# A graph layer's edge loop: three tiles of every eighth group copied by columns, in place of one tile of 200 groups

## The chip, the cores and the metric

The kernel runs on one core of a Trainium2 chip. The metric is the time of one execution on the device, in microseconds. The core's engines work side by side, each through a queue of its own in order: PE (matrix products and transposes; PEld is its weight load), DVE (vector work), ACT (scalar work, activations, copies), POOL (here it issues the indirect gathers) and SP (it issues most of the plain transfers). An engine waits for another through semaphores.

## The reference

One message-passing layer with a residual and a layer norm, on 12500 nodes of 64 values and 212500 edges with 32 values each, all in float32. The edges are sorted by their target `dst`.

```python
msg_in = concatenate([x[src], x[dst], edge_attr], axis=-1)      # 64 + 64 + 32
messages = relu(msg_in @ mW1 + mb1) @ mW2 + mb2                 # hidden 128, out 64
aggregated = segment_sum(messages, dst, 12500)
upd_in = concatenate([x, aggregated], axis=-1)
y = x + relu(upd_in @ uW1 + ub1) @ uW2 + ub2
out = (y - mean(y)) / sqrt(var(y) + 1e-5)                       # over the 64 values
```

## The kernel before

**Groups and steps.** The edges are cut into 554 groups of 384 (`GE`), three tiles of 128 each; the last group has 148 edges in two tiles, so there are 1661 tiles. A group goes through three parts, a step or two apart. In `turn`, the rows of `x` that the group's edges point to, which lie one edge per partition in a ring slot `own_s` (20 slots, `RING`), are transposed on PE (L398) into PSUM, and ACT copies the result (L409) into `own_st`, where a group has 384 columns, one per edge: 64 rows of features, then 32 rows of a one-hot that says where in a window of 32 targets the edge belongs; the edge's own values are loaded below these. `hidden` multiplies by the weights (L424, PE) and DVE takes the relu (L435). `sums` adds the group's messages up by target (L452, L457, PE), and DVE adds them to the running sums (L466, L467). Step k is one bundle on PE of turn k, hidden k - 2 and sums k - 4, with one set of waits ahead of it and one signal behind it; in the last ten steps (`SHORT`) the three parts go apart and catch up. As targets are finished, chunks of 512 nodes go through the update (L473 to L521), one piece after each `sums`, the last chunk behind the last group.

**Two ways for the source rows.** Most tiles are fetched from HBM by an indirect DMA that POOL issues, one per tile (`gather`, L165 to L177). It is written 16 steps ahead of its group and may start as soon as ACT has copied the group that had the slot 20 groups earlier (`marks_by`, L672 and L679, holds what its first and later gathers wait for). For some tiles there is no gather. The node features lie transposed in SBUF (`own_xc`), and each edge's column of 64 values is copied from there to its place in `own_st` by an instruction of its own, on ACT (L572) or DVE (L570), with an address that was read into a register (L549). From step 18 (`BEGIN`) on, each step copies 48 columns (`COLS`): 20 on DVE, 28 on ACT. `COPIED` (L87 to L89) lists the groups so served: with 128 columns each there are 200 of them, the first 21, the last 552, one every 2.67 steps. In such a group the first tile comes by columns and the other two are gathered, so ACT's copy of it is two instructions: 32 rows (the one-hot) of the first 128 columns, and all 96 rows of the other 256.

**Order around the change.** In step k, ACT copies turn k, then 28 columns in three parts of 12, 8 and 8, each behind a load of its addresses. DVE does its additions, 5 and 7 and 8 columns, the one-hot of a later group and the relu. The columns of a group are finished in the step before its turn; `hidden`, two steps later, waits for them (L428). The first column of a group on each engine waits until the group that had the place in `own_st` 12 groups earlier has gone through `hidden` (L575).

Of the kernel before, what the change touches and what calls it, by code (L numbers as in the profile page):

```python
# [14 lines left out]
AF = mybir.ActivationFunctionType  # L15
# [5 lines left out]
P = 128  # L21
N = 12500
E = 212500
D = 64
# [5 lines left out]
W = 32  # L30
TG = 3
GE = TG * P
G = (E + GE - 1) // GE
# [14 lines left out]
SHORT = 10  # L48
LEAD = 6
TIMES = 4  # L50
BEGIN = 18
# [3 lines left out]
COLS = sum(VCOLS + ACOLS)  # L55
SPAN = 8
# [3 lines left out]
def tiles_of(g):  # L60

    n = min(GE, E - g * GE)
    return [min(P, n - j * P) for j in range((n + P - 1) // P)]
# [21 lines left out]
TABLE = [(b, min(4, (NP - b) // P)) for b in range(0, NP, CH)]  # L85
FIRST_FREE = 6 + len(TABLE) - 1
COPIED = []  # L87
while BEGIN - (-P * (len(COPIED) + 1) // COLS) < G - 1:
    COPIED.append(BEGIN - (-P * (len(COPIED) + 1) // COLS))  # L89


class Own:
# [23 lines left out]
def ordered(ctx: ExitStack, tc: tile.TileContext, a, own, ok):  # L116
# [3 lines left out]
    nc = tc.nc  # L120
# [20 lines left out]
    columned = set(COPIED)  # L141

    def after(first, *others):

        tc.declare_no_dep(first.ins, group="quiet", reason="waits for the last of a step")
        for i in others:
            tc.add_manual_dep(
                first.ins, i.ins.name,
                mybir.DependencyInfo(mybir.DependencyClass.Sync, mybir.DependencyReason.DATA),
                reason="the kernel's own rings",  # L150
            )
        return first
# [3 lines left out]
    def ordered_by_steps(i):  # L156

        engine = i.ins.engine
        tc.declare_no_dep(i.ins, group="features", keep=before.get(engine, []),
                          reason="TensorE's step has read what the last turn of the ring wrote")  # L160
        tc.add_to_no_dep_group("features", i.ins)
        before[engine] = [i.ins]
        return i

    def gather(g):  # L165
        s = own.s[g % RING]
        loads[g] = [
            nc.gpsimd.indirect_dma_start(  # L168
                out=s[:p, j, :D], out_offset=None, in_=x[:, :],
                in_offset=bass.IndirectOffsetOnAxis(  # L170
                    ap=src_sb[:p, g * TG + j : g * TG + j + 1], axis=0),
            )
            for j, p in enumerate(tiles_of(g)) if j or g not in columned
        ]
        marks = marks_by.pop(g - RING, [])
        for n, i in enumerate(loads[g]):
            after(i, *marks[: n + 1][-1:])  # L177
# [7 lines left out]
    for g in range(AHEAD):  # L185
        gather(g)
# [105 lines left out]
    starts, rows_at, indices, columns_by = {}, {}, {}, {}  # L292
# [46 lines left out]
    def columns(g):  # L339
        t, c = own.st[g // SB % BLOCKS], (g % SB) * GE  # L340
        return t, c, sum(tiles_of(g))
# [50 lines left out]
    def turn(g, ps):  # L392


        s = own.s[g % RING]
        xt = ps[0][: D + W, :GE]
        did = [
            nc.tensor.transpose(xt[:, j * P : j * P + p], s[:p, j, :], ident[:p, :p])  # L398
            for j, p in enumerate(tiles_of(g))
        ]  # L400

        def copy(step):
            t, c, n = columns(g)
            turn_by[g] = step
            whole = [(slice(D + W), slice(n))]
            apart = [(slice(D, D + W), slice(P)), (slice(D + W), slice(P, n))]
            copies = [
                ordered_by_steps(
                    after(nc.scalar.activation(t[r, c : c + n][:, m], xt[r, m], AF.Copy), step))  # L409
                for r, m in (apart if g in columned else whole)  # L410
            ]
            if g >= BLOCKS * SB:
                after(copies[0], hidden_by[g - BLOCKS * SB])
            copy_by[g] = copies
            return copies

        return did, [*loads.pop(g), places_by[g]], copy
# [104 lines left out]

    def indexes(i):

        n = min(SPAN * COLS, P * len(COPIED) - i * SPAN * COLS)
        if n > 0:
            indices[i] = ixp.tile([1, SPAN * COLS], I32, name="index")
            nc.sync.dma_start(indices[i][:, :n], a["src_copied"][:, i * SPAN * COLS :][:, :n])

    def addresses(i):  # L530

        if i in indices:
            t = indices[i][:, : min(SPAN * COLS, P * len(COPIED) - i * SPAN * COLS)]
            nc.vector.tensor_scalar(t, t, 4.0, float(own.at), ALU.mult, ALU.add)

    def registers(k, *parts):

        i, n = divmod(k - BEGIN, SPAN)
        if i < 0:
            return  # L540
        all_parts = [*((ET.DVE, c) for c in VCOLS), *((ET.Activation, c) for c in ACOLS)]
        for part in parts:
            engine, count = all_parts[part]
            c0 = (k - BEGIN) * COLS + sum(c for _, c in all_parts[:part])
            count = min(count, P * len(COPIED) - c0)
            if count <= 0:
                return
            b = c0 - i * SPAN * COLS
            _, v = nc.values_load_multi_w_load_instructions(  # L549
                indices[i][0:1, b : b + count], engines=[engine],  # L550
                min_val=own.at, max_val=own.at + 4 * (N - 1),
                skip_runtime_bounds_check_because="a source is one of the nodes",
            )
            held[part] = engine, c0, v

    def fetch(part, first=None):

        engine, c0, v = held.pop(part, (None, 0, ()))
        if first and v[first:]:
            held[part] = engine, c0 + first, v[first:]  # L560
            v = v[:first]
        for q, at in enumerate(v, c0):
            g, c = COPIED[q // P], q % P
            t, first_c, _ = columns(g)
            o = t.bitcast(U8)[:D, 4 * (first_c + c) : 4 * (first_c + c + 1)]
            x_at = xc_bytes[:D, bass.ds(at - own.at, 4)]
            by = columns_by.setdefault(g, {})
            new = engine not in by
            if engine == ET.DVE:
                by[engine] = nc.vector.tensor_copy(o, x_at)  # L570
            else:
                by[engine] = nc.scalar.activation(o, x_at, AF.Copy)  # L572
            last[engine] = by[engine]
            ordered_by_steps(after(by[engine],
                                   *([hidden_by[g - BLOCKS * SB]] if new else [])))  # L575
# [49 lines left out]
    inputs(1)  # L625
    relative(NEAR_GROUPS, G)
    indexes(0)
    made = summed = 0
    between, held, last = [], {}, {}

    for k in range(G):
# [6 lines left out]
        if k == CHECKED:  # L638
            addresses(0)
            combined()  # L640
            ordered_edges()
            early.close()
            up = ctx.enter_context(tc.tile_pool(name="upd", bufs=2))
# [4 lines left out]
        if k < G - SHORT:  # L648
            between.append(lambda: registers(k, 0))
            step((turn, k), *([(hidden, k - 2)] if k > 1 else []),  # L650
                 *([(sums, k - 4)] if k > 3 else []))
            made, summed = max(0, k - 1), max(0, k - 3)
            if between:
                between.pop()()
        else:

            step((turn, k))
            for _ in range(2):
                if summed < made:
                    step((sums, summed))  # L660
                    summed += 1
            for _ in range(2):
                if made <= k:
                    step((hidden, made))
                    made += 1
            registers(k, 0)
        fetch(0, FIRST)
        registers(k, 1)
        fetch(0)
        window(k + SB)  # L670
        onehot(k + LEAD)
# [346 lines left out]
```

## Time and profile before

| | |
|---|---|
| median of 3 runs | 1869.42 us (1865.05 to 1871.72) |
| profiled execution, its own time | 1870.53 us |
| its span, first to last instruction | 1868.8 us |
| TensorE's granted clock, mean | 0.974 of full speed |
| column copies on ACT / on DVE | 14924 / 10676 |
| DMA, mean busy share between 200 and 1800 us | 0.23 |

How to read it: "busy" counts the time in which an engine has an instruction in work. Loads of registers and the issue of plain DMAs are not counted. A group of instructions carries its line in the kernel, the engine, the tile written and read, the count, the busy time, the mean duration of one, and the idle time of the engine ahead of it with the releaser that the profile infers. Instructions overlap on their engine, so that a column copy with a mean of 192 ns costs ACT about 99 ns (1472.5 us for 14924).

### The profile page before, as it was taken

The numbers are of one execution on the slowest core, as the hardware profiler recorded it, in microseconds if no ns is written. First come the engines' busy times: TensorE is split into PE (matmuls) and PEld (weight loads), VectorE is DVE, ScalarE is ACT, GpSimd is POOL, SyncE is SP. The second block draws the span as 40 slices with busy tenths as digits, with TensorE's granted clock in tenths as the row PEclk, the third lists the DMA queues.
The fourth block names the chain that finished last, engine by engine and source line by source line (L and its number), as shares of the span: only waits on it lengthen the run. The fifth ranks groups of instructions, "written<-read, shape, count | busy, mean of one in ns | idle before, by whom it ended". The sixth has DMA issues, their size and how long they took to land. (4 is left out here: it accounts for less than half of the span.)

```text
span 1868.8 us, 64939 instructions
## 1 busy us (share of the span) xinstructions
PE 1336.8 (72%) x12323; PEld 1171.3 (63%) x12323; DVE 1537.9 (82%) x13355; ACT 1752.3 (94%) x15772; POOL 1386.4 (74%) x1468
## 2 busy tenths in 40 slices
PE   5767767777677677677676776777766767767776
PEld 4766656666666566566665666666656656656665
DVE  4558888888888888888888888888888888888885
ACT  3379999999999999999999999999999999999994
POOL 7777777777777777777777777777777777777771
PEclk9889999999999999999999999999999999999998
DMA  5532222222222222222222222222222222222220
GB/s 143 142 97 61 45 55 54 45 53 51 49 54 45 54 50 50 53 50 50 51 52 50 49 50 49 53 51 49 53 47 53 48 52 53 46 54 49 50 51 15
DMA packets 112209, 103.99 MB, mean 56 GB/s; under 512 B 51267, under 2 KB 82642, under 8 KB 111794
## 3 DMA queue, kind: packets, MB, share of 16 engines
q0 software_dynamic: 46752, 47.94, 13.4%
q1 hardware_dynamic: 64198, 51.31, 10.2%
q14 instruction: 311, 2.55, 0.4%
q8 instruction: 104, 1.70, 0.4%
q10 hardware_dynamic: 844, 0.48, 0.1%
HBM read 89.97 MB, written 9.62 MB: 53 GB/s over the span
## 5 line engine op out<-in xcount | busy, mean ns | idle before, releaser
L168 POOL DMA_INDIRECT own_s<-in_x,src_sb x1461 | 1385.6, 948 | 446.7 <-DMA own_s<-in_x,src_sb 182.7
L572 ACT ACTIVATE own_st<-own_xc 64x4 uint8 x14924 | 1472.5, 192 | 3.1 <-DMA by_dst<-t 3.0
L570 DVE COPY own_st<-own_xc 64x4 uint8 x10676 | 970.6, 187 | 149.9 <-issue 125.0
L398 PE MATMUL own_ps<-own_ident,own_s 128*96 128x128 f32 x1661 | 298.4, 290 | 452.0 <-ACT own_st L409 427.7
L398 PEld LDWEIGHTS own_ps<-own_ident,own_s 128*96 128x96 f32 x1661 | 166.5, 130 | 524.9 <-ACT own_st L409 490.9
L452 PE MATMUL own_ps<-own_s,own_h 128*128 128x128 f32 x3322 | 474.8, 280 | 6.2 <-DVE own_h L435 5.6
L424 PE MATMUL own_ps<-own_wm,own_st 128*128 128x128 f32 x3322 | 477.0, 281 | 2.1 <-ACT own_st L409 1.7
L452 PEld LDWEIGHTS own_ps<-own_s,own_h 128*128 128x128 f32 x3322 | 428.0, 197 | 8.9 <-DVE own_h L435 7.6
L424 PEld LDWEIGHTS own_ps<-own_wm,own_st 128*128 128x128 f32 x3322 | 428.7, 197 | 3.6 <-ACT own_st L409 1.9
L409 ACT ACTIVATE own_st<-own_ps 96x384 f32<-96x384 f32 (+2 forms) x754 | 301.4, 400 | 55.5 <-PE own_ps L457 22.0
L435 DVE TENSOR_SCALAR own_h<-own_ps 128x384 f32<-128x384 f32 x553 | 299.8, 542 | 56.1 <-PE own_ps L457 45.7
L457 PE MATMUL own_ps<-own_s,own_one 128*1 128x32 f32 x3322 | 187.9, 193 | 0.0
L457 PEld LDWEIGHTS own_ps<-own_s,own_one 128*1 128x1 f32 x3322 | 113.1, 83 | 68.3 <-issue 3.1
L466 DVE TENSOR_TENSOR own_agg<-own_ps,own_agg 128x32 f32 x554 | 101.1, 183 | 62.4 <-DVE own_h L435 36.9
L386 DVE TENSOR_TENSOR own_s<-iota,dlc 128x96 f32<-128x96 f32 x554 | 136.4, 247 | 0.4
L467 DVE TENSOR_TENSOR own_xc<-own_ps,own_xc 1x32 f32 x554 | 102.1, 184 | 31.6 <-PE u_ps L478 13.2
L490 PE MATMUL u_ps<-same,own_xc 65*128 65x64 f32 (+1 forms) x196 | 40.9, 292 | 26.1 <-ACT u L483 26.1
L360 PE MATMUL u_ps<-w1b,own_xc 65*128 65x128 f32 x196 | 33.3, 321 | 32.3 <-DMA own_xc<-in_xT 12.8
L360 PEld LDWEIGHTS u_ps<-w1b,own_xc 65*128 65x128 f32 x196 | 28.4, 223 | 34.9 <-issue 20.5
L490 PEld LDWEIGHTS u_ps<-same,own_xc 65*128 65x128 f32 (+1 forms) x196 | 31.1, 199 | 29.5 <-ACT u L483 29.4
L363 ACT ACTIVATE t<-u_ps 128x512 f32<-128x512 f32 (+1 forms) x25 | 14.7, 589 | 30.7 <-PE u_ps L360 16.3
L492 PE MATMUL u_ps<-u,u 128*128 128x64 f32 (+1 forms) x196 | 40.8, 293 | 0.0
(59 smaller groups left out, 266.1 us busy)
## 6 DMA issues: line engine op xcount, KB each, us to landing
own_st<-in_efT SPq DMA_DIRECT2D x138, 192.0 KB
own_s<-in_x,src_sb POOLq DMA_INDIRECT x1461
own_wm<-by_dst SPq DMA_DIRECT2D x554, 16.0 KB
by_dst<-t SPq DMA_DIRECT2D x24, 256.0 KB
out<-o SPq DMA_DIRECT2D x24, 128.0 KB
own_xc<-in_xT SPq DMA_DIRECT2D x12, 179.2 KB
index<-in_src_copied SPq DMA_DIRECT2D x66, 1.5 KB
dlc_i<-in_dst_cols SPq DMA_DIRECT2D x1, 807.0 KB
```

Of the source, the lines that this page charges most:

```text
L168: nc.gpsimd.indirect_dma_start(out=s[:p, j, :D], out_offset=None, in_=x[:, :], in_offset=bass.IndirectOffsetOnAxis(ap=src_sb[:p, g * TG + ...
L386: places_by[g] = nc.vector.tensor_tensor(own.s[g % RING][:, :, D:], iota.unsqueeze(1).to_broadcast([P, TG, W]), dlc[:, g * TG : (g + 1) * ...
L398: nc.tensor.transpose(xt[:, j * P : j * P + p], s[:p, j, :], ident[:p, :p])
L409: after(nc.scalar.activation(t[r, c : c + n][:, m], xt[r, m], AF.Copy), step))
L424: nc.tensor.matmul(pre[:p, j, :], t[:, c + j * P : c + j * P + p], wm[g % NW], start=True, stop=True)
L435: relu_by[g] = [nc.vector.tensor_scalar(h, pre, 0.0, None, ALU.max)]
L452: did.append(nc.tensor.matmul(sg, h[:p, j, :], s[:p, j, D:].unsqueeze(1).to_broadcast([p, TIMES, W]), start=j == 0, stop=j == len(sizes) - 1))
L457: did.append(nc.tensor.matmul(counted, own.one[:p], s[:p, j, D:], start=j == 0, stop=j == len(sizes) - 1))
L466: a = after(nc.vector.tensor_tensor(agg[:, at], sg[:, 0, :], agg[:, at], ALU.add), step)
L467: return [a, after(nc.vector.tensor_tensor(count, counted, count, ALU.add), step)]
L570: by[engine] = nc.vector.tensor_copy(o, x_at)
L572: by[engine] = nc.scalar.activation(o, x_at, AF.Copy)
```

## The change

The list `COPIED` is now made for whole groups: 384 columns each, so with 48 columns a step one group every eight steps. There are 65 of them, 26, 34, 42 and so on to 538, since the list now stops ahead of the last ten steps. Such a group has no gather at all, and ACT's copy of it is one instruction, 32 rows of the one-hot by 384 columns. PE transposes the slot's old contents with it, and nothing reads the result. The counts of addresses follow.

```diff
 COPIED = []
-while BEGIN - (-P * (len(COPIED) + 1) // COLS) < G - 1:
-    COPIED.append(BEGIN - (-P * (len(COPIED) + 1) // COLS))
+while BEGIN - (-GE * (len(COPIED) + 1) // COLS) < G - SHORT:
+    COPIED.append(BEGIN - (-GE * (len(COPIED) + 1) // COLS))
...
-            for j, p in enumerate(tiles_of(g)) if j or g not in columned
+            for j, p in enumerate(tiles_of(g)) if g not in columned
...
-            whole = [(slice(D + W), slice(n))]
-            apart = [(slice(D, D + W), slice(P)), (slice(D + W), slice(P, n))]
-            copies = [
-                ordered_by_steps(
-                    after(nc.scalar.activation(t[r, c : c + n][:, m], xt[r, m], AF.Copy), step))
-                for r, m in (apart if g in columned else whole)
-            ]
+            r = slice(D if g in columned else 0, D + W)
+            copies = [ordered_by_steps(
+                after(nc.scalar.activation(t[r, c : c + n], xt[r, :n], AF.Copy), step))]
...
-        n = min(SPAN * COLS, P * len(COPIED) - i * SPAN * COLS)
+        n = min(SPAN * COLS, GE * len(COPIED) - i * SPAN * COLS)
...
-            g, c = COPIED[q // P], q % P
+            g, c = COPIED[q // GE], q % GE
...
-        "src_copied": np.concatenate([v["src"][g * GE :][:P] for g in COPIED])[None],
+        "src_copied": np.concatenate([v["src"][g * GE :][:GE] for g in COPIED])[None],
```

More of the change, by code (lines that the diff above doesn't have):

```diff
@@ L532, in addresses @@
         if i in indices:
-            t = indices[i][:, : min(SPAN * COLS, P * len(COPIED) - i * SPAN * COLS)]
+            t = indices[i][:, : min(SPAN * COLS, GE * len(COPIED) - i * SPAN * COLS)]
             nc.vector.tensor_scalar(t, t, 4.0, float(own.at), ALU.mult, ALU.add)
@@ L544, in registers @@
             c0 = (k - BEGIN) * COLS + sum(c for _, c in all_parts[:part])
-            count = min(count, P * len(COPIED) - c0)
+            count = min(count, GE * len(COPIED) - c0)
             if count <= 0:
```

## The prediction

> **What bounds the kernel now.** I read the page's busy shares and costliest groups first, then POOL's timeline, then ACT's groups by shape, then the end of the timeline.
>
> ```profile
> PE 1336.8 (72%) x12323; PEld 1171.3 (63%) x12323; DVE 1537.9 (82%) x13355; ACT 1752.3 (94%) x15772; POOL 1386.4 (74%) x1468
> ...
> L168 POOL DMA_INDIRECT own_s<-in_x,src_sb x1461 | 1385.6, 948 | 446.7 <-DMA own_s<-in_x,src_sb 182.7
> L572 ACT ACTIVATE own_st<-own_xc 64x4 uint8 x14924 | 1472.5, 192 | 3.1 <-DMA by_dst<-t 3.0
> ```
>
> By this ACT is the bound (94%), and POOL, at 74%, seems to have a quarter of its time free. POOL's timeline says otherwise. Columns: start, duration, what, and in brackets the idle time before.
>
> ```profile
> 3.03 1.15 POOL L168 DMA_INDIRECT own_s<-in_x,src_sb  x1 [1.44 <-DMA src_sb<-in_src]
> ...
> 8.23 0.94 POOL L168 DMA_INDIRECT own_s<-in_x,src_sb  x1 [0.30 <-issue]
> 9.48 1.47 POOL L168 DMA_INDIRECT own_s<-in_x,src_sb  x1 [0.30 <-issue]
> ...
> 1000.27 0.95 POOL L168 DMA_INDIRECT own_s<-in_x,src_sb  x1 [0.30 <-DMA own_s<-in_x,src_sb]
> 1001.52 0.95 POOL L168 DMA_INDIRECT own_s<-in_x,src_sb  x1 [0.30 <-issue]
> ...
> 1832.96 0.90 POOL L168 DMA_INDIRECT own_s<-in_x,src_sb  x1 [0.30 <-issue]
> ```
>
> The idle 0.30 us stands before every gather, whatever is named as its releaser, so 446.7 us of idle is 1461 x 0.306: a fixed part of a gather, not waiting. One gather costs 1.25 us (1001.52 - 1000.27), from 3 us to 1833.86 us without a hole: POOL is full too. The stretches confirm it (columns: stretch, length, busy time and count, then TensorE's granted clock, DMA share, GB/s):
>
> ```profile
> 0.00:200.00 200.00, 149.68 (x156) 0.94 0.43 107
> 200.00:1800.00 1600.00, 1210.25 (x1279) 0.98 0.23 51
> ```
>
> 1600 / 1279 = 1.251 us a gather. Now ACT, by shape, between 200 and 1800 us, and the count of its copies ahead of 200 us:
>
> ```profile
> L572 ACT ACTIVATE own_st<-own_xc 64x4 uint8 x13768 | 1358.1, 192 | 0.1
> L409 ACT ACTIVATE own_st<-own_ps 96x384 f32<-96x384 f32 x307 | 149.1, 486 | 10.5 <-issue 9.7 <-PE own_ps L457 0.2
> L409 ACT ACTIVATE own_st<-own_ps 96x256 f32<-96x256 f32 x184 | 70.0, 380 | 2.2
> L409 ACT ACTIVATE own_st<-own_ps 32x128 f32<-32x128 f32 x184 | 49.3, 268 | 8.6 <-issue 5.7 <-PE own_ps L457 0.2
> ...
> L409 ACT ACTIVATE own_st<-own_ps x57: 268/487/489, 16.9 to 199.3; 96x384 f32<-96x384 f32 x37, 32x128 f32<-32x128 f32 x10, 96x256 f32<-96x256 f32 x10
> ```
>
> ACT does 307 + 184 = 491 steps in 1600 us, 3.259 us each. Those 491 groups, 184 of them with one tile copied by columns, need 491 x 3 - 184 = 1289 gathers; POOL made 1279. So POOL is slightly slower than ACT and lives on a lead: by 200 us 156 gathers are issued, while the 47 steps done need 47 x 3 - 10 = 131, so it is 25 gathers or 31 us ahead. Who waits tells that the lead is never used up:
>
> ```profile
> PE own_ps L398 <- ACT own_st L409: 427.7, 412, 2.0
> ...
>   PE own_ps L398: 0.4, 1
> ```
>
> The first row is PE's turn waiting for ACT, 427.7 us in all; the second is the whole of PE's waiting for a gather: once, 0.4 us. At the end, too, the last data are there well before they are wanted:
>
> ```profile
> 13.18 0.84 PE L398 MATMUL own_ps<-own_ident,own_s 128*96 128x128 f32 x3 [0.41 <-DMA own_s<-in_x,src_sb]
> ...
> 1853.67 0.42 PE L398 MATMUL own_ps<-own_ident,own_s 128*96 128x128 f32 x2
> 1854.13 0.29 ACT L409 ACTIVATE own_st<-own_ps 96x148 f32<-96x148 f32 x1 [2.41 <-PE own_ps L398]
> 1854.38 0.56 DVE L435 TENSOR_SCALAR own_h<-own_ps 128x384 f32<-128x384 f32 x1
> 1854.99 0.94 PE L452 MATMUL own_ps<-own_s,own_h 128*128 128x128 f32 x6 [0.90 <-DVE own_h L435]
> ...
> 1856.12 0.81 PE L424 MATMUL own_ps<-own_wm,own_st 128*128 128x128 f32 x4
> ...
> 1863.43 0.52 ACTq L519 DMA_DIRECT2D out<-o  x1
> ```
>
> The one turn that waits starts at 13.18 us, and the gather it waits for (9.48 + 1.47) ends on POOL at 10.95: data land 2.2 us after POOL's bar ends. So group 553 is in SBUF at 1833.86 + 2.2 = 1836.1 us, and its turn starts at 1853.67, 17.6 us later. The kernel before is paced by ACT, with POOL a few microseconds behind it as the next bound.
>
> **The change part by part.**
>
> *Gathers.* Fewer tiles are copied: 65 x 3 = 195 in place of 200. POOL therefore issues 1661 - 195 = 1466 gathers, five more. Where they go shows in POOL's order; own_s6 and own_s7 are the ring slots of groups 26 and 27, and the brackets hold the semaphores waited for: DMASW of earlier gathers, Activation of ACT. Before:
>
> ```order
> L168 DMA own_s6<-in_x,src_sb_81 128x64 [waits DMASW4_49,Activation_49]
> L168 DMA own_s6<-in_x,src_sb_81 128x64 [waits DMASW5_49]
> L168 DMA own_s7<-in_x,src_sb_81 128x64 [waits DMASW6_49,Activation_49]
> L168 DMA own_s7<-in_x,src_sb_81 128x64 [waits DMASW7_49]
> L168 DMA own_s7<-in_x,src_sb_81 128x64 [waits DMASW0_49]
> ```
>
> And now:
>
> ```order
> L168 DMA own_s5<-in_x,src_sb_81 128x64 [waits DMASW3_49,Activation_49]
> L168 DMA own_s5<-in_x,src_sb_81 128x64 [waits DMASW4_49]
> L168 DMA own_s5<-in_x,src_sb_81 128x64 [waits DMASW5_49]
> L168 DMA own_s7<-in_x,src_sb_81 128x64 [waits DMASW6_49,Activation_49]
> L168 DMA own_s7<-in_x,src_sb_81 128x64 [waits DMASW7_49]
> ```
>
> Slot 6 is skipped: every eighth group needs nothing of POOL, the seven between need 21 gathers, 26.3 us. Per group that is the old 2.625 gathers, 3.284 us. The waits are of the old kinds: a gather's first waits for ACT's copy 20 groups back, and with a lead of some ten groups that copy is long done. POOL's end moves by 5 x 1.25 = 6.3 us, to **1840.1 us**, and the last data land at 1842.3.
>
> *ACT's copies.* In 200 groups the pair 128 + 256 (268 + 380 = 648 ns) gives way to one copy of 384 elements; the new ones are 32 x 384, which no row shows. The four shapes above lie on one line in the length (128: 268, 256: 380, 384: 486) although the first has 32 partitions and the others 96, so I take 486 ns. Bounds: 486 - 110 if fewer partitions helped, 648 if nothing is gained; in the sum they matter little, as follows. Saved: 0.162 us x 184 = 29.8 us between 200 and 1800 us, so ACT alone would do a step in (1600 - 29.8) / 491 = 3.198 us. POOL needs 3.284. The difference, 0.086 us x 491 = 42 us, is more than the usable lead: 31 us, less 2.2 for landing, some 2.6 for PE's step ahead of ACT's copy and 2.5 for two gathers that now come before group 26, makes 24. **So the lead is gone after about 24 / 0.086 = 280 steps, near 1.1 ms, and from there POOL paces the kernel.** It is exhausted by 1800 us for any saving over 0.06 us a pair.
>
> *Columns.* 48 a step as before, on the same engines; 24960 in place of 25600, and they end after step 537 instead of 551. ACT's order at the end, before:
>
> ```order
> L572 ACTIVATE own_st<-own_xc 64x4 x8
> L409 ACTIVATE own_st<-own_ps 96x384 [waits PE_49]
> L506 ACTIVATE rstd<-mv,eps 128x4 [waits DVE_49]
> L409 ACTIVATE own_st<-own_ps 32x128 [waits PE_49]
> L409 ACTIVATE own_st<-own_ps 96x256
> L409 ACTIVATE own_st<-own_ps 96x148 [waits PE_49]
> ```
>
> And now:
>
> ```order
> L568 ACTIVATE own_st<-own_xc 64x4 x8
> L407 ACTIVATE own_st<-own_ps 32x384 [waits PE_49]
> L407 ACTIVATE own_st<-own_ps 96x384 [waits PE_49] x10
> L479 ACTIVATE u<-u_ps 128x512 [waits Activation_49]
> L407 ACTIVATE own_st<-own_ps 96x384 [waits PE_49] x3
> ```
>
> The last 15 steps have copies alone on ACT. They need 44 gathers, 3.757 us a step. PE's own work for a step, and for a chunk of the update, of which one falls in there:
>
> ```profile
> L398 PE MATMUL own_ps<-own_ident,own_s 128*96 128x128 f32 x1661 | 298.4, 290 | 452.0 <-ACT own_st L409 427.7
> ...
> L452 PE MATMUL own_ps<-own_s,own_h 128*128 128x128 f32 x3322 | 474.8, 280 | 6.2 <-DVE own_h L435 5.6
> L424 PE MATMUL own_ps<-own_wm,own_st 128*128 128x128 f32 x3322 | 477.0, 281 | 2.1 <-ACT own_st L409 1.7
> ...
> L457 PE MATMUL own_ps<-own_s,own_one 128*1 128x32 f32 x3322 | 187.9, 193 | 0.0
> ...
> L490 PE MATMUL u_ps<-same,own_xc 65*128 65x64 f32 (+1 forms) x196 | 40.9, 292 | 26.1 <-ACT u L483 26.1
> ...
> L492 PE MATMUL u_ps<-u,u 128*128 128x64 f32 (+1 forms) x196 | 40.8, 293 | 0.0
> ```
>
> A step is (298.4 + 474.8 + 477.0 + 187.9) / 554 = 2.6 us, so each gather-paced step leaves 1.1 us. Of the chunk that becomes ready at group 546 the second half alone is (40.9 + 40.8) / 25 = 3.3 us; I take the first half at no more. Six steps of spare (6.9 us) just cover these 6.6. I take no backlog, with 0 to 4 us as bounds. The missing columns cost nothing to anyone: PE and DVE wait for data there.
>
> *The drain.* Before, from the last turn (1853.67) to the end of the span (1868.8) is 15.1 us. Of it 0.9 us is the bracket before the sums at 1854.99, waiting for a relu that DVE did late; paced by gathers that relu is done earlier. I take 14.4 to 15.1.
>
> *Sum.* 1833.86 + 6.3 + 2.2 + 14.4 to 15.1 = 1856.8 to 1857.5 span. The profiled execution took 1870.53 for a span of 1868.8, so 1.7 is added: 1858.5 to 1859.2, that is 11.3 to 12 us under its own time, and 10 to 11 under the median 1869.42 of the three runs. **Forecast 1859.** ACT's 30 us of saved copies mostly don't show, because POOL cannot follow.
>
> **The rivals.**
>
> (a) ACT's pair is no cheaper joined, or the saved time goes elsewhere. Then ACT keeps its pace up to step 538, whose copy starts here:
>
> ```profile
> 1800.73 0.66 ACT L409 ACTIVATE own_st<-own_ps 32x128 f32<-32x128 f32 x2
> ```
>
> Fifteen more steps at the old 3.26 us give the last copy at 1849.6; from the old last copy (1854.13) to the end are 14.7: span 1864.3, time 1866. For it: the waits' bracket "issue" shows gaps on ACT that the shapes don't explain. Against it: they are 18 us over 491 steps.
>
> (b) POOL can go faster than it did, and the whole ACT saving shows: 1800.7 less 194 pairs x 0.162 = 1769, 15 steps at 3 us, 14.7 and 1.7: 1831. Against it: neither 0.95 nor 0.30 varies anywhere. The Trainium skill, page "SBUF — State Buffer", section "SBUF: two separate sides", holds that a DVE copy in a two-port mode locks GpSimd out of writing descriptors and gives about 620 ns for such a DMA alone; by it the 44 gathers beside no columns would gain up to 0.33 us each, an estimate of 14 us. The trace doesn't bear it out: the gather at 8.23 us, before any column, takes 0.94 us, as at 1000 us.
>
> (c) Slower. POOL has run ahead of the step all along; if the skipped group made it hold until that group's step is over, because a ring slot or mark is bound to it, each period would last 26.3 + 3.2 us. From 1.1 ms on that is 30 periods or 95 us: 1955. It decides at the fourth hold (11.5 us). Against it: the order shows no new kind of wait, and the slots waited for are 20 groups old.
>
> (d) The gathers pace it but the tail piles up: the update chunk leaves its 4 us, or the data land later than 2.2 us. 1863.
>
> **How the numbers follow.** Forecast 0.66, (a) 0.13, (b) 0.04, (c) 0.06, (d) 0.11. The range, 1855 to 1866, holds the forecast, (d) and about half of (a). A measurement of this kernel tells 0.3%, 5.6 us, from no change, so faster means under 1863.8: the forecast, (b), most of (d): 0.79. Same: most of (a) and some of (d): 0.14. Slower: (c) and a corner of (a): 0.07.
>
> **What would show it.** POOL: 1466 gathers at 1.25 us, the last ending near 1840. PE's turn waiting for the gathers (0.4 us before) by over a hundred microseconds, starting near 1 ms. ACT busy less than 98% of the second half, with no idle in the first. A 32x384 copy of about 486 ns. The last turn at 1842 to 1843. It is wrong if POOL shows idle gaps over 0.3 us, if the turn still waits for ACT alone to the end, or if the last turn starts later than 1846.

## The result, and the profile after

The changed kernel takes 1853.93 us (median of four runs, 1853.06 to 1854.97) beside 1869.08 us before (four runs, 1865.05 to 1871.72): a ratio of 0.9924, 95% interval 0.9908 to 0.9939. That is 15.1 us less. The forecast was 1859 with a range of 1855 to 1866: the direction is right, the time falls 1.1 us below the range. The profiled execution took 1853.82 us for a span of 1852.1 us. One thing has to be known for the tables further down: in some sets of runs the kernel before itself took 2488 to 2542 us, with gaps between the small instructions of ACT and DVE that its own profile does not have, and no conclusion here rests on a time of those sets.

The page's busy shares and costliest groups, after (two lines lower in places: L407 is the old L409, L568 the old L572, L453 the old L457):

```profile
PE 1316.0 (71%) x12323; PEld 1157.7 (63%) x12323; DVE 1515.1 (82%) x13077; ACT 1691.2 (91%) x15208; POOL 1387.1 (75%) x1473
...
L168 POOL DMA_INDIRECT own_s<-in_x,src_sb x1466 | 1386.3, 946 | 447.9 <-DMA own_s<-in_x,src_sb 226.5
L568 ACT ACTIVATE own_st<-own_xc 64x4 uint8 x14560 | 1437.2, 192 | 4.9 <-DMA by_dst<-t 3.0
L407 ACT ACTIVATE own_st<-own_ps 96x384 f32<-96x384 f32 (+1 forms) x554 | 268.2, 484 | 98.0 <-PE own_ps L453 48.0
```

The row of the same copies in the page of before:

```profile
L409 ACT ACTIVATE own_st<-own_ps 96x384 f32<-96x384 f32 (+2 forms) x754 | 301.4, 400 | 55.5 <-PE own_ps L457 22.0
```

POOL makes the 1466 gathers and still looks three quarters busy. ACT fell from 94% to 91%. Its idle time ahead of the copies, 98.0 us where it was 55.5, is the new thing; 48.0 of it is put down to one line of PE. The windows of ACT say where (stretch, length, busy time and count, clock, DMA share, GB/s):

```profile
200.00:1000.00 800.00, 787.26 (x7251) 0.99 0.21 51
1000.00:1800.00 800.00, 766.43 (x7042) 0.99 0.21 51
```

ACT is busy for 98.4% of the first stretch and 95.8% of the second: in the second half it waits for somebody. The waits of PE's turn, first between 200 and 1000 us, then, behind the dots, between 1000 and 1800 us (total, times, longest):

```profile
PE own_ps L398 <- ACT own_st L407: 203.2, 206, 1.9
...
PE own_ps L398 <- DMA own_s<-in_x,src_sb: 57.6, 42, 1.8
PE own_ps L398 <- ACT own_st L407: 49.5, 44, 2.1
PE own_ps L398 <- DVE own_xc L463: 43.0, 31, 2.0
```

In the first stretch no wait for a gather is listed. In the second the gathers lead the list of the turn's waits. The last row names a DVE addition; a wait for several things is put down to one of them, so the 57.6 us need not be all that the gathers cost (the part on the prediction counts it another way). PE's timeline shows the change of hands (start, duration, idle before and what ended it):

```profile
1116.45 0.53 PE L398 MATMUL own_ps<-own_ident,own_s 128*96 128x128 f32 x3 [1.22 <-ACT own_st L407]
1120.24 0.51 PE L398 MATMUL own_ps<-own_ident,own_s 128*96 128x128 f32 x3 [1.64 <-DMA own_s<-in_x,src_sb]
```

At 1120 us a turn waits for a gather, the first after the program's start that the profile puts down to one. And ACT's copies some fifty steps later:

```profile
1304.86 0.49 ACT L407 ACTIVATE own_st<-own_ps 96x384 f32<-96x384 f32 x1
1308.59 0.49 ACT L407 ACTIVATE own_st<-own_ps 96x384 f32<-96x384 f32 x1 [0.59 <-PE own_ps L453]
1312.31 0.49 ACT L407 ACTIVATE own_st<-own_ps 96x384 f32<-96x384 f32 x1 [0.57 <-PE own_ps L453]
```

They come 3.73 us apart, three gathers of 1.25 us, and ACT stands idle ahead of them. The end of the timeline, POOL's last gathers, PE's last turns and the last store:

```profile
1832.37 0.94 POOL L168 DMA_INDIRECT own_s<-in_x,src_sb  x1 [0.30 <-ACT rstd L502]
1833.62 0.94 POOL L168 DMA_INDIRECT own_s<-in_x,src_sb  x1 [0.30 <-issue]
1834.86 0.90 POOL L168 DMA_INDIRECT own_s<-in_x,src_sb  x1 [0.30 <-DMA own_s<-in_x,src_sb]
...
1831.08 0.50 PE L398 MATMUL own_ps<-own_ident,own_s 128*96 128x128 f32 x3 [0.30 <-DMA own_s<-in_x,src_sb]
1834.81 0.51 PE L398 MATMUL own_ps<-own_ident,own_s 128*96 128x128 f32 x3 [1.31 <-DMA own_s<-in_x,src_sb]
1837.09 0.43 PE L398 MATMUL own_ps<-own_ident,own_s 128*96 128x128 f32 x2
...
1846.94 0.52 ACTq L515 DMA_DIRECT2D out<-o  x1
```

POOL ends at 1834.86 + 0.90 = 1835.76. The last turn starts 1.33 us behind it, where before it came 17.6 us behind the landed data. The turn at 1834.81 waits for the gather at 1832.37, the last of its group, whose bar ends at 1833.31: the turn starts 1.5 us later. The last turn shows no idle ahead of it: its data came just as PE's own work of the step before was done, so 1.33 us is the most that the last landing can have taken.

### The profile page after: what moved, and what is told of

Read it like the earlier page. It is cut to its first block, busy times and chain, and to the rows that moved or that the text cites. A ratio compares the mean times of both kernels' runs of the same rounds, so it can differ in the third digit from the quotient of the medians.

```text
span 1852.1 us, 64089 instructions
## 1 busy us (share of the span) xinstructions
PE 1316.0 (71%) x12323; PEld 1157.7 (63%) x12323; DVE 1515.1 (82%) x13077; ACT 1691.2 (91%) x15208; POOL 1387.1 (75%) x1473
## 5 line engine op out<-in xcount | busy, mean ns | idle before, releaser
L568 ACT ACTIVATE own_st<-own_xc 64x4 uint8 x14560 | 1437.2, 192 | 4.9 <-DMA by_dst<-t 3.0
L566 DVE COPY own_st<-own_xc 64x4 uint8 x10400 | 943.8, 186 | 145.3 <-issue 119.4
L398 PE MATMUL own_ps<-own_ident,own_s 128*96 128x128 f32 x1661 | 291.3, 285 | 473.4 <-ACT own_st L407 258.2
L420 PE MATMUL own_ps<-own_wm,own_st 128*128 128x128 f32 x3322 | 471.0, 279 | 0.0
L420 PEld LDWEIGHTS own_ps<-own_wm,own_st 128*128 128x128 f32 x3322 | 423.0, 195 | 1.3 <-issue 0.5
L407 ACT ACTIVATE own_st<-own_ps 96x384 f32<-96x384 f32 (+1 forms) x554 | 268.2, 484 | 98.0 <-PE own_ps L453 48.0
L453 PE MATMUL own_ps<-own_s,own_one 128*1 128x32 f32 x3322 | 187.3, 193 | 0.0
L453 PEld LDWEIGHTS own_ps<-own_s,own_one 128*1 128x1 f32 x3322 | 112.6, 83 | 67.8 <-issue 2.2
L486 PEld LDWEIGHTS u_ps<-same,own_xc 65*128 65x128 f32 (+1 forms) x196 | 30.1, 193 | 18.9 <-ACT u L479 18.1
```

Source lines behind the costliest of these rows:

```text
L407: after(nc.scalar.activation(t[r, c : c + n], xt[r, :n], AF.Copy), step))]
L420: nc.tensor.matmul(pre[:p, j, :], t[:, c + j * P : c + j * P + p], wm[g % NW], start=True, stop=True)
L453: did.append(nc.tensor.matmul(counted, own.one[:p], s[:p, j, D:], start=j == 0, stop=j == len(sizes) - 1))
```

## The experiments

The theory: from about 1.1 ms on the count of POOL's gathers sets the time, so a gather less is worth 1.25 us and the length of ACT's copies is worth nothing in the end. The main rival: ACT and the early end of the columns make the time, and the waits for gathers lie beside it.

**Fourteen gathers fewer.** The changed kernel, without the third gather of every fortieth group; the edges concerned use the slot's old contents.

```diff
-            for j, p in enumerate(tiles_of(g)) if g not in columned
+            for j, p in enumerate(tiles_of(g)) if g not in columned and (j < 2 or g % 40 != 31)
```

> As stated for the same kernel before, now on its own: theory P (POOL paces the second half and sets the end) 14 x 1.25 = 17.5 us under 1853.9, 1836.4 us; rival A (gathers hidden) within 2 us of 1853.9. If the kernel before runs near 2500 us again, neither is tested.

Measured: 1835.89 us (1835.13 to 1836.65) beside 1868.98 before, ratio 0.9823 (0.9795 to 0.9852). That is 18.0 us under the changed kernel, 1.29 us for each gather left out. The whole of the turn's waiting for gathers in this kernel's waits, and the end of its timeline:

```profile
PE own_ps L398 <- DMA own_s<-in_x,src_sb: 6.1, 5, 2.0
...
1816.80 0.90 POOL L168 DMA_INDIRECT own_s<-in_x,src_sb  x1 [0.30 <-issue]
...
1817.10 0.50 PE L398 MATMUL own_ps<-own_ident,own_s 128*96 128x128 f32 x3 [0.49 <-DMA own_s<-in_x,src_sb]
1819.24 0.42 PE L398 MATMUL own_ps<-own_ident,own_s 128*96 128x128 f32 x2
```

The waits shrink from 62.9 to 6.1 us, and yet the last turn still starts 1.54 us behind POOL's last bar, close to the 1.33 of the changed kernel. The end moved with POOL's end, which comes 18.1 us earlier (1817.70 in place of 1835.76). The theory holds.

**Forty-two gathers fewer**, to find where POOL's hold ends (the third gather of every twelfth group from 49 on is left out, and those edges use old contents too).

```diff
-            for j, p in enumerate(tiles_of(g)) if g not in columned
+            for j, p in enumerate(tiles_of(g)) if g not in columned and (j < 2 or g < 40 or g % 12 != 1)
```

> As for the same kernel before, with what is known since: 14 gathers fewer gave 1835.9, and PE's turn waited for a gather 6.1 us in all. Theory P: POOL would allow 42 x 1.25 = 52.5 us less, 1801, but ACT is the next bound: at its 3.21 us a step the copy of step 538 comes at about 1774, 15 steps at 3 us, 16.4 behind: 1830 to 1836 us, hardly under the 14, and no wait for a gather. If ACT's pace itself depended on the gathers (their data or their marks): 1801 to 1825.

Measured: 1829.77 us (1829.22 to 1830.33) beside 1871.28, ratio 0.9782 (0.9753 to 0.9812). The further 28 gathers, 35 us of POOL's time, brought only 6.1 us. POOL's last gather, and ACT's copy of the last group by columns, in step 538:

```profile
1782.81 0.90 POOL L168 DMA_INDIRECT own_s<-in_x,src_sb  x1 [0.30 <-DMA own_s<-in_x,src_sb]
...
1774.29 0.99 ACT L407 ACTIVATE own_st<-own_ps 32x384 f32<-32x384 f32 x2
```

POOL is done 45 us before the span's end and the turn waits for a gather once in the whole run, 0.5 us. Here ACT, and behind the last columns PE, set the time again. So without POOL's limit the change would take the kernel to about 1830, 39 us under before; POOL's limit takes 24 of them back.

**The copies cut in two again**, in the changed kernel: 128 and 256 elements, in the 200 groups that had the pair before.

```diff
+PAIRED = [BEGIN - (-P * (i + 1) // COLS) for i in range(200)]
...
-            copies = [ordered_by_steps(
-                after(nc.scalar.activation(t[r, c : c + n], xt[r, :n], AF.Copy), step))]
+            cuts = [slice(P), slice(P, n)] if g in PAIRED else [slice(n)]
+            copies = [
+                ordered_by_steps(
+                    after(nc.scalar.activation(t[r, c : c + n][:, m], xt[r, m], AF.Copy), step))
+                for m in cuts
+            ]
```

> As stated for the same kernel before. Theory P: ACT is back at 3.26 us a step, slower than POOL to step 538, so the lead lasts; 1857 to 1866 us, and no turn waits for a gather before 1.7 ms. If POOL alone sets the time whatever ACT does: 1854. If joining the pair were worth its full 30 us: 1884.

Measured: 1854.34 us (1853.75 to 1854.93) beside 1868.84, ratio 0.9921 (0.9893 to 0.995): the same as the changed kernel, and under the 1857 to 1866 that were expected. ACT's copies by shape between 200 and 1000 us, of this kernel and, behind the dots, of the changed one (count, busy, mean ns):

```profile
L410 ACT ACTIVATE own_st<-own_ps 96x384 f32<-96x384 f32 x155 | 75.3, 486 | 5.6 <-issue 4.0 <-PE own_ps L458 0.4
L410 ACT ACTIVATE own_st<-own_ps 96x256 f32<-96x256 f32 x62 | 23.0, 371 | 0.0
L410 ACT ACTIVATE own_st<-own_ps 96x128 f32<-96x128 f32 x62 | 16.9, 272 | 2.2 <-issue 1.9
L410 ACT ACTIVATE own_st<-own_ps 32x256 f32<-32x256 f32 x31 | 11.1, 359 | 0.0
```

```profile
L407 ACT ACTIVATE own_st<-own_ps 96x384 f32<-96x384 f32 x219 | 106.2, 485 | 9.9 <-issue 7.2 <-PE own_ps L453 0.8
L407 ACT ACTIVATE own_st<-own_ps 32x384 f32<-32x384 f32 x31 | 14.9, 481 | 0.9 <-issue 0.2
```

The cut kernel does 155 + 62 + 31 = 248 steps in 800 us, 3.226 us each, the changed one 219 + 31 = 250, 3.20 us each. Over 93 cuts in 248 steps that is some 0.07 us a cut, but one step more or less in the count would change it by 0.03. From the start of a step's copy to the start of the next, the mean over the same stretch is 3.222 us in the cut kernel and 3.209 in the changed one, 0.034 us a cut; by medians, a step behind a pair takes 3.146 us and a plain one 3.085, a difference of 0.06. So a cut costs 0.03 to 0.06 us, where the prediction had 0.162. One stretch of the cut kernel's ACT shows why (the row with x2 is the pair, 0.54 us from the first start to the second end):

```profile
601.85 0.49 ACT L410 ACTIVATE own_st<-own_ps 96x384 f32<-96x384 f32 x1
...
604.92 0.49 ACT L410 ACTIVATE own_st<-own_ps 96x384 f32<-96x384 f32 x1
...
608.03 0.54 ACT L410 ACTIVATE own_st<-own_ps 96x128 f32<-96x128 f32 x2
...
611.16 0.49 ACT L410 ACTIVATE own_st<-own_ps 96x384 f32<-96x384 f32 x1
```

A pair takes 0.54 us where the single copy takes 0.49: the second of two copies overlaps the first, and the two durations, 272 and 371 ns, don't add. The steps are 3.07, 3.11 and, with the pair, 3.13 us. And the slower ACT takes longer to use up POOL's lead, as the theory has it; this kernel's first turn that waits for a gather, after the start:

```profile
1331.05 0.50 PE L399 MATMUL own_ps<-own_ident,own_s 128*96 128x128 f32 x3 [1.27 <-DMA own_s<-in_x,src_sb]
```

It comes at 1331 us in place of 1120 (not before 1.7 ms was expected, since the cut was priced too high), and the end is the same. What ACT does ahead of that point shifts the point and not the end.

**The early end alone.** The kernel before, one tile of a group by columns as ever, with the list of groups ended ten steps sooner.

```diff
-while BEGIN - (-P * (len(COPIED) + 1) // COLS) < G - 1:
+while BEGIN - (-P * (len(COPIED) + 1) // COLS) < G - SHORT:
```

> The kernel before with one edit: its list of copied groups stops ahead of the last ten steps as in the change (196 groups, 1465 gathers, columns to step 540), one tile each and ACT's two copies as before. Theory P: ACT keeps its 3.25 us to step 540 (1810 us), PE then takes 12 steps at about 3 us from data already there, 16.4 behind: about 1863, some 6 us of the 15. If the early end is the whole gain: 1854. If it brings nothing: 1869.

Measured: 1859.69 us (1858.26 to 1861.14) beside 1870.43, ratio 0.9942 (0.9911 to 0.9973). That is 10.7 us saved, a good two thirds of the change's 15. PE's turns near the end, and POOL's last gather:

```profile
1803.80 0.53 PE L398 MATMUL own_ps<-own_ident,own_s 128*96 128x128 f32 x3 [0.94 <-ACT own_st L409]
1806.89 0.53 PE L398 MATMUL own_ps<-own_ident,own_s 128*96 128x128 f32 x3 [0.95 <-ACT own_st L409]
1808.96 0.53 PE L398 MATMUL own_ps<-own_ident,own_s 128*96 128x128 f32 x3
...
1839.28 0.49 PE L398 MATMUL own_ps<-own_ident,own_s 128*96 128x128 f32 x3
1841.99 0.42 PE L398 MATMUL own_ps<-own_ident,own_s 128*96 128x128 f32 x2
...
1833.17 0.89 POOL L168 DMA_INDIRECT own_s<-in_x,src_sb  x1 [0.30 <-DMA own_s<-in_x,src_sb]
```

The last steps with columns are 3.09 us long in these lines (3.25 on the mean between 200 and 1000 us). Without columns the next turns follow back to back on PE, first 2.07 us apart; in the last ten steps, whose parts go apart and which hold a chunk of the update, they are 2.7 to 4.5 us apart. Over the 13 steps from 1806.89 to 1841.99 the mean is 2.70 us. The data for them are there, since POOL's lead is not used up: no turn's wait in this kernel is put down to a gather, and the last turn comes 7.9 us behind POOL's last bar. Those 7.9 us less the 1.3 of landing are what ACT's faster steps could still take, and in the changed kernel took, before POOL stopped them.

**The kernel before once more**, for POOL's spacing in another execution.

> The kernel before, unchanged, a second profile, for the spacing of POOL's gathers: 1.2509 us in its first profile, 1.2486 in the changed kernel's and in those of its two variants so far. If the 2.3 ns belong to the program, 1.2509 again and POOL's end near 1834 us; if the first profile's chip or hour was the odd one, 1.2486 and POOL's end near 1830.5. Time 1865 to 1872 in either case, since ACT paces this kernel.

Measured: 1868.49 us, span 1866.7. Its last gather:

```profile
1830.94 0.90 POOL L168 DMA_INDIRECT own_s<-in_x,src_sb  x1 [0.30 <-issue]
```

In the first profile of the same kernel it started at 1832.96. The table holds the first and the last start on POOL's timeline in each profile, and their distance divided by the number of gathers less one:

| profile | gathers | first start | last start | mean spacing, us |
|---|---|---|---|---|
| before | 1461 | 3.03 | 1832.96 | 1.2534 |
| before once more | 1461 | 2.96 | 1830.94 | 1.2520 |
| early end alone | 1465 | 2.91 | 1833.17 | 1.2502 |
| changed kernel | 1466 | 2.91 | 1834.86 | 1.2505 |
| copies cut again | 1466 | 2.92 | 1835.60 | 1.2510 |
| fourteen fewer | 1452 | 2.90 | 1816.80 | 1.2501 |
| forty-two fewer | 1424 | 3.01 | 1782.81 | 1.2507 |

The expectations state 1.2509 and 1.2486 us for the first profiles of before and of the changed kernel; over the whole run, as in the table, it is 1.2534 and 1.2505. The spacing differs between two executions of one program by 0.0014 us, 2.0 us over the whole run. The two of before lie above all others. The early end has the same tiles and copies as before and a low spacing, so it isn't the way the groups are served that makes the difference; what does was not found.

**A step of 50 columns**, tried as a faster kernel: ten columns in DVE's second part in place of eight, so 67 groups by columns and 1460 gathers.

```diff
-VCOLS = (12, 8)
+VCOLS = (12, 10)
```

> As for the same kernel before, whose set ran with the kernel before at 2494 us and gaps of up to 2 us between instructions. Theory P: POOL ends 6 x 1.25 = 7.5 us earlier than in the changed kernel, 1846 us. If DVE has no room for two more columns: 1854 or more.

Measured: 2929.52 us beside 1871.48, ratio 1.5654 (1.5608 to 1.5699). A miss by over a thousand microseconds. This kernel's waits, and a stretch of its DVE with, behind the dots, the same place of a step in the changed kernel:

```profile
DVE own_st L566 <- issue: 699.1, 528, 2.5
ACT own_st L568 <- issue: 511.0, 523, 1.7
DVE own_agg L462 <- issue: 487.0, 267, 3.0
...
1502.11 0.59 DVE L566 COPY own_st<-own_xc 64x4 uint8 x7 [1.96 <-issue]
```

```profile
1002.28 0.67 DVE L566 COPY own_st<-own_xc 64x4 uint8 x7 [0.25 <-issue]
```

The gaps of up to 3 us stand ahead of copies and additions that are no longer than before, and the profile names no releaser for them. The trace's records of the loads of addresses into registers (L545), which the views leave out, show where they come from: such a load takes 1.75 us on the mean on DVE and 1.34 on ACT, in the changed kernel 0.73 and 0.63. The order of the instructions differs only in the counts. Why two more addresses a step should cost this is open. Their number alone is not it: with four more (52 columns, further down) the loads take 0.85 and 0.63 us. That kernel ran only in a set that the result's section puts aside, but in such a set the kernel before has its usual 0.73 and 0.63 us a load. That an index block's rows are 200 bytes apart with 50 columns, and 192 with 48, is a guess and was not tried.

**Left open.** Two kernels ran only in the sets that the result's section sets aside: 52 columns a step (2557.47 beside 2494.3) and the changed kernel with its list running to the end again (2579.18 beside 2530.89).

> The changed kernel with four more columns a step on DVE (52 in place of 48; 70 groups copied, 15 gathers fewer). Theory P: POOL ends 15 x 1.25 = 18.7 us earlier, near 1817, which would give 1835; ACT's own pace gives about 1837; DVE, with 4 x 0.09 us more in a step of about 2.8, stays under 3.2: 1836 to 1842. Rival A, or DVE already at its limit: no faster than 1853.

> The changed kernel with the old end of the list: 66 whole groups, the last 546, columns to step 545, 1463 gathers, three fewer. Theory P: POOL, which sets the end, stops 3 x 1.25 = 3.75 us earlier, and ACT's and DVE's columns in seven more steps lie beside waiting: 1850 us. If it is the early end of the columns that matters, as it did with one tile a group (10.7 us for ending 11 steps earlier), the last steps are slow again: 1856 to 1860.

Neither settles anything, so the whole groups without the early end have no time of their own. Earlier runs of the kernels above fell in such sets too; what was expected of each, and the times:

The kernel before once more, twice:

> The kernel before, unchanged, in a second execution, for the spacing of POOL's gathers: 1.2509 us in its first profile, 1.2486 us in the changed kernel's. If the 2.3 ns belong to the execution (chip, hour), a second profile shows some other spacing, near 1.2486, and POOL ends near 1830.5 us; if they belong to the program, it shows 1.2509 again and POOL ends near 1834. Time 1865 to 1872 in either case, since ACT paces this kernel.

> The kernel before, unchanged, once more, since the set before this one ran at 2536 us with gaps between ACT's instructions and says nothing of a gather's spacing. As stated for that run: spacing near 1.2486 us and POOL's end near 1830.5 if the 2.3 ns belong to the execution, 1.2509 and 1834 if they belong to the program; 1865 to 1872 us.

Fourteen gathers fewer, three times:

> The changed kernel without the third gather of 14 groups (31, 71, and so on every 40 to 551), which then use what the slot held; nothing else is left out. Theory P, POOL paces the second half and sets the end: 14 x 1.25 = 17.5 us less, 1836.4 us. Rival A, the gain came from ACT's joined copies and the early end of the columns and the gathers are still hidden: within 2 us of 1854.

> As stated for the same kernel in the set before: theory P (POOL paces the second half and sets the end) 14 x 1.25 = 17.5 us under the changed kernel, 1836.4 us; rival A (gathers hidden) within 2 us of 1854. If the gaps between instructions are there again (2536 us before), neither is tested.

> The changed kernel without the third gather of 14 groups (31, 71, and so on every 40 to 551), which then use what the slot held; nothing else is left out. Theory P, POOL paces the second half and sets the end: 14 x 1.25 = 17.5 us under 1853.9, 1836.4 us. Rival A, the gathers are hidden and the gain came from ACT and the early end of the columns: within 2 us of 1853.9.

Forty-two gathers fewer, twice:

> The changed kernel without the third gather of 42 groups (every twelfth, 49 to 541). Theory P: POOL would allow 42 x 1.25 = 52.5 us less, 1801 us, but ACT is the next bound: 194 pairs joined at 0.162 us take the copy of step 538 from 1800.7 to 1769, 15 steps at 3 us, 14.7 and 1.7 behind: 1831 us, and PE's turn waits for no gather. Rival A: within 2 us of 1854.

> The changed kernel without the third gather of 42 groups (every twelfth, 49 to 541). Theory P: POOL would allow 42 x 1.25 = 52.5 us less, 1801 us, but ACT is the next bound. At the changed kernel's pace ahead of its first wait for a gather (step 1 at 16.7 us, step 340 at 1138 us; 3.21 us a step from step 40 on) the copy of step 538 comes at about 1776, 15 steps at 3 us, 16.4 behind: 1837 us, and PE's turn waits for no gather. Rival A: within 2 us of 1853.9.

The copies cut again, the early end alone, and 50 columns a step:

> The changed kernel with ACT's copy cut in two again (128 and 256 columns) in the 200 groups that had the pair before; gathers and columns as changed. Theory P: ACT is back at 3.26 us a step, slower than POOL to step 538, so the lead lasts; the copy of step 538 comes at 1800.7 as before, the last 15 steps without columns take 40 to 48 us, then 16.4: 1857 to 1866, and no turn waits for a gather before 1.7 ms. If POOL alone sets the time whatever ACT does: 1854. If joining the pair were worth its full 30 us: 1884.

> The kernel before with one edit: its list of copied groups stops ahead of the last ten steps as in the change (196 groups, 1465 gathers, columns to step 540), one tile each and ACT's two copies as before. Theory P: ACT keeps its 3.25 us to step 540 (1810 us), PE then takes 12 steps at about 3 us from data already there, 16.4 behind: about 1863, some 6 us of the 15. If the early end is the whole gain: 1854. If it brings nothing: 1869.

> The changed kernel with two more columns a step on DVE (50 in place of 48; 67 groups copied, 1460 gathers, six fewer). Theory P: POOL ends 6 x 1.25 = 7.5 us earlier and the kernel with it, 1846 us; ACT's own limit (1830 with 42 gathers fewer) is further off, and DVE, busy 2.73 us a step and idle for about 0.23 between its instructions, has room for 2 x 0.09. If DVE has no room, its relu comes later and PE with it: 1854 or more.

| kernel | time | before beside it | run again above |
|---|---|---|---|
| before once more | 2533.14 and 2494.82 | 2536.2 and 2495.51 | yes |
| fourteen fewer | 2564.28, 2523.83 and 2526.3 | 2536.2, 2495.51 and 2494.3 | yes |
| forty-two fewer | 2536.91 and 2503.29 | 2536.2 and 2494.3 | yes |
| copies cut again | 2581.6 | 2536.2 | yes |
| early end alone | 2487.32 | 2494.3 | yes |
| 50 columns | 3001.11 | 2494.4 | yes |

In them every kernel with whole groups by columns came out level with before or up to 2.4% slower, with 50 columns 20% slower, and only the early end alone a little faster. None of the kernels that compute the whole layer beat the changed one.

## Why the prediction was right in its mechanism and missed in size

**POOL is full, and its lead runs out near 1.1 ms: right.** The gathers stand 0.30 us apart from the first to the last, the first wait that the profile puts down to one is at 1120 us, and taking 14 gathers away moved the end by 18 us where the sum says 17.5. The cut copies and the fourteen missing gathers moved the point where POOL takes over, and that is what a lead does.

**ACT at 3.198 us a step: 3.20 measured, and so near by luck.** By the count of copies between 200 and 1000 us it is 3.20; from copy start to copy start it is 3.209 there and 3.253 before, so 0.044 us a step were saved where 29.8 / 491 = 0.061 were forecast. The price that was wrong is the "0.162 us x 184", the durations of the pair added up, although the two copies overlap. The cut costs 0.03 to 0.06 us, and cutting the copies again took 0.013 of the 0.044 back. The larger part of the saving lay in the steps around a copy of 32 rows, for which the prediction had no term. In the changed kernel's ACT:

```profile
1002.35 0.49 ACT L407 ACTIVATE own_st<-own_ps 96x384 f32<-96x384 f32 x1
1002.73 2.76 ACT L568 ACTIVATE own_st<-own_xc 64x4 uint8 x28
1005.51 0.48 ACT L407 ACTIVATE own_st<-own_ps 32x384 f32<-32x384 f32 x1
1006.02 2.77 ACT L568 ACTIVATE own_st<-own_xc 64x4 uint8 x28
1008.82 0.49 ACT L407 ACTIVATE own_st<-own_ps 96x384 f32<-96x384 f32 x1
```

The step into such a copy takes 3.16 us, the one behind it 3.31, against 3.08 for a plain step (median of 187 between 200 and 1000 us): some 0.3 us for a group served by columns, although the copy itself takes no longer (481 ns, forecast 486). The lines show where it goes. The columns behind the plain copy start at 1002.73, before it ends at 1002.84. The copy of 32 rows starts only when the columns ahead of it have ended (1005.49), the columns behind it only when it has ended (1005.99), and so does the next plain copy (1008.79). In that stretch a plain copy starts 0.07 us before the end of the columns ahead of it and overlaps those behind it by 0.10 us (medians of 188), while at these three places there is a gap of 0.02 us instead: 0.09 + 0.12 + 0.09 = 0.30 us. Why ACT does not overlap there is not settled.

Before, by the same medians, the two steps took 3.16 and 3.26 us, 0.26 us a group, the pair's cut included. Eight steps held three such groups before and hold one now: 3 x 0.26 - 0.31 = 0.47 us in eight steps, 0.059 a step by these medians. So the change makes ACT faster mainly because fewer groups are touched, and less because copies are joined.

**The waits for gathers, over a hundred microseconds: right, though the list of waits names only 62.9 us.** The trace also records when each gather's data signal that they have landed. Between 1120 and 1800 us, 123 of the 208 turns start within 0.4 us behind the signal of their group's last gather, with 176.7 us of idle on PE ahead of them, whatever the list names as the releaser. Between 200 and 1000 us no turn does; with fourteen gathers fewer 13 turns do between 1120 and 1800 us, and with forty-two fewer none. PE was idle ahead of its turns before that too, waiting for ACT (207 us in 250 turns between 200 and 1000 us, 209 us in 208 turns between 1120 and 1800): the gathers have mostly taken ACT's place.

**The sum.** The miss against the sum's 1856.8 is 4.7 us of span, and all of it lies ahead of the last turn, which was to start at 1842 to 1843 and started at 1837.09:

| term | forecast | measured |
|---|---|---|
| POOL's end before | 1833.86 | 1833.86 and, once more, 1831.84 |
| POOL's end after | 1840.1 | 1835.76 |
| landing (POOL's end to the last turn) | 2.2 | 1.3 |
| last turn to the end of the span | 14.4 to 15.1 | 15.0 |
| span | 1856.8 to 1857.5 | 1852.1 |

The step that failed is POOL's end, "moves by 5 x 1.25" from the 1833.86 us of one profile: 1840.1 us was forecast, 1835.76 measured. The five gathers were counted rightly; the base they were added to came from one execution, and its spacing was treated as exact. The prediction says of a gather's two parts that "neither 0.95 nor 0.30 varies anywhere". The 0.30 hardly does, but single bars do, as the 1.47 us in the prediction's own lines show; and so does the typical bar. POOL's gathers (shortest, median and longest in ns), before and after:

```profile
L168 POOL DMA_INDIRECT own_s<-in_x,src_sb x1461: 902/947/1651, 3.0 to 1833.0; - x183
...
L168 POOL DMA_INDIRECT own_s<-in_x,src_sb x1466: 902/944/1470, 2.9 to 1834.9; - x184
```

0.003 us times 1465 gathers is 4.2 us, nearly the whole 4.3. The second profile of before (median 945 ns) accounts for 2.0 of it. The other 2.3 are the difference between that second profile's spacing and the changed kernel's, and stay open. With POOL's end at 1835.76 and every other term as forecast, the time would have been 1854.1 to 1854.8 us: this step alone puts it under the range.

The second term is the landing: 2.2 us came from the program's sixth gather, at 9.48 us. The trace's signals put the landing at 1.45 us behind the bar on the median between 200 and 1800 us, and at 2.07 in the first 50 us. In the first 200 us the DMA share is 0.41, later 0.21; that the traffic makes this difference was only argued. The range had no term for a variation of the spacing; with 2 us for it, the low end would have been 1853.

**The early end.** Rival (a), where ACT keeps its pace, was priced at 1866 with fifteen more steps "at the old 3.26 us". That pace is the wrong one: without columns ACT does not pace, and the 13 steps of the kernel with the early end alone took 2.70 us each on the mean. (The prediction's 2.6 us for PE's own work adds busy times that overlap; a step that is one bundle takes 2.07, and the rest is the last ten steps with their chunk of the update.) That kernel took 1859.7. It doesn't matter for the forecast, in which POOL sets the end, but it halved the distance between the two cases, so the time alone could not have told them apart.

**The other rivals.** (b), a POOL that goes faster, gave 1831 on ACT's side; with POOL out of the way the chip gives 1829.8, so the price was good and the condition false. The last gathers, beside no column copies at all, take the same 0.94 us (1832.37, 1833.62). By the Trainium skill, page "SBUF — State Buffer", section "SBUF: two separate sides", a DVE copy in a two-port mode keeps GpSimd from writing descriptors; nothing of that is seen in these bars. In which mode the column copies run no run shows. (c), POOL held at the skipped group, is refuted: no gather there has more than 0.32 us ahead of it. (d), the pile-up in the tail, did not come: the last three turns start 3.73 and 2.28 us apart, no slower than three and two gathers take.

## What to carry to other kernels

An engine with the same short gap ahead of each of its instructions may be full, whatever its busy share says, as POOL was here at 75%: multiply count by spacing and set it against the span, for every queue, before a change makes the busiest engine faster. A bound that runs on a lead is priced by where the lead is used up, and behind that point only its own count matters. And when such a product of some 1500 equal terms decides, take the spacing from more than one execution, since here a quarter of a per cent of it was as wide as the range given below the forecast.

## What the runs showed of the hardware that was not expected

- The spacing of back-to-back indirect gathers of 128 rows of 256 bytes is nearly fixed, 1.2501 to 1.2534 us on average over a run, yet differs by 2.0 us in a whole run between two executions of one program. Single bars take 0.89 to 1.68 us.
- Two copies of 128 and 256 elements on ACT take 0.54 us where one of 384 takes 0.49, although they are listed with 272 and 371 ns.
- A copy of 32 rows among copies of 96 rows is no longer itself, but the steps around it are some 0.3 us longer in all: the overlaps of 0.07 and 0.10 us that a plain copy has with its neighbours are missing at three places.
- With ten columns in place of eight in one part of the step, the loads of addresses into registers take 1.75 us on the mean on DVE in place of 0.73, and the kernel takes 2930 us where the kernel before, beside it, takes 1871.
